# A two-layer convolution and attention network on one core: the bias network's last layer on tiles of eight keys by sixteen sums

## The chip, the cores and the metric

The kernel runs on one core of a Trainium2 chip. The metric is device time in microseconds. Three runs of the kernel before gave 2735.99 to 2738.67 us, median 2737.09. The profile is of one execution, with a span of 2735.9 us. Everything is float32.

## The reference, cut to what matters

The input is x of shape (2, 512, 32, 32). Layer 0 is deformable attention with 8 heads (16 pairs of batch and head, called groups below), each with 1024 queries and 64 keys, followed by an MLP. Layer 1 is full attention over 1024 positions. What the change touches is the bias that a small network makes for each query and key of layer 0:

```python
pos = grid_q[:, :, None, :] - grid_kv[:, None, :, :]
bias = jnp.sign(pos) * jnp.log1p(jnp.abs(pos))
bias = jax.nn.relu(bias @ cpb_w1 + cpb_b1)             # 2 -> 128
bias = jax.nn.relu(bias @ cpb_w2 + cpb_b2)             # 128 -> 128
bias = (bias @ cpb_w3 + cpb_b3).reshape(b, GROUPS, H * W, Hd * Wd)   # 128 -> 1
sim = jnp.einsum('bhid,bhjd->bhij', qh, kh) + bias
attn = jax.nn.softmax(sim, axis=-1)
```

It runs for 16 x 1024 x 64 pairs of query and key. The positions of the keys come from offsets: a 6 x 6 depthwise convolution of the queries, a GELU, a small product and a tanh.

## The kernel before, in words

**Engines.** PE is TensorE, DVE is VectorE, ACT is ScalarE, POOL is GpSimd, SP is the queue that issues most loads. Each works through its own instructions in order and waits on semaphores. The order on each engine is made by a scheduler from the order of the program; `issue_after` holds an instruction back until a named one has been issued.

**Head.** Constants are loaded on ACT's queue (kp, L170, holds an identity, W2 and w3), x on SP's. The first chunk (a chunk is 128 channels of one batch, two heads) is normalised on ACT (L235), multiplied by the query weights (psq, L243), copied to qa (L248), and its 36 taps of the depthwise convolution run on DVE (L280, L282). PE multiplies the weights of layer 1 together meanwhile (psg, L499). On POOL, `swap` (L190 to L222) reorders the columns of W2 and the entries of w3 by sign, in some 60 small steps, and makes cw2, sc and w3s.

**The loop** (L718) has 256 slots, each of four keys of one group; 16 slots make a group. In a slot:

- `st_layer1` (L585) makes h, 128 hidden channels by 4 keys by 1024 queries, on DVE (L593), up to three slots ahead, as there are three buffers.
- `st_layer2` (L603) multiplies h by W2 on PE (L610), in four parts z of 32 output channels. Each of four column groups of PE has one of the four keys, so a part is a PSUM tile of 4 keys x 32 channels by 1024 queries; there are three such tiles. ACT evicts each with bias and ReLU: parts 0 and 2 to rx (L616), 1 and 3, scaled by w3, to ua and ub (L618).
- `st_sum` (L624) forms rx * w3 + ua and rx * w3 + ub on DVE (L626). Then a DMA with addition, on POOL's queue (L628), adds ub into ua. So ua has, for each of 4 keys, 32 partial sums.
- `st_layer3` (L630) runs after every second slot for the two slots before: a matmul with w3s (L649) adds the 32 partial sums of each key into the rows of sim, a PSUM tile that a group fills in 8 such calls. At the last call of a group the product of queries and keys is added (L640).

After the last call of a group, `softmax_steps` (L657) goes on a step per slot on ACT, DVE and PE.

**Beside the loop** a generator `later` (L455) makes the features of the other seven chunks, one step per slot: `chain` (L226) computes the offsets (taps on ACT, L290, `TAPS` of them per step, and L305 on DVE) and stores their features to DRAM (fdr, L369); `sample` (L377) gathers keys and values, and writes the keys to kvz (L431 to L441). `load_tables` (L559) reads a group's features for 16 keys back from DRAM, broadcast over the partitions (fb, one buffer), every fourth slot, and `st_tables` (L570) makes two tables of them on ACT. The tables of a chunk can be loaded once its features are stored.

**After the loop** come the output projection, the MLP and layer 1 (L764 on), almost all on PE.

Of the kernel before, what the change touches and what calls it, by code (L numbers as in the profile page):

```python
# [8 lines left out]
F32 = mybir.dt.float32  # L9
AF = mybir.ActivationFunctionType  # L10
ALU = mybir.AluOpType
AX = mybir.AxisListType
PSUM = bass.MemoryType.PSUM

P = 128
# [5 lines left out]
NSL = 16  # L21
KT = 16
LAST = 2
KS = 6
# [3 lines left out]
HEAD = 3  # L28
TAPS = [36, 6, 6, 4, 4]
NU = 4  # L30
# [6 lines left out]
    ("bq", 4), ("bv", 4), ("bp", 4), ("dwb", 1), ("cb1", 1), ("cb3", 1),  # L37
    ("w1x", 1), ("w1y", 1), ("cb2", 4), ("w3", 4), ("dww", 36),
]
# [8 lines left out]
@with_exitstack  # L48
def conv_seq_kernel(ctx: ExitStack, tc: tile.TileContext, x, xt, kst, cst, vec, wsm, outw, w1, w2, wl, out):
    nc = tc.nc  # L50


    cp = ctx.enter_context(tc.tile_pool(name="cp", bufs=1))
    kp = cp.tile([P, 384], F32, name="kp")
    vs = cp.tile([P, NV], F32, name="vs")
    nc.scalar.dma_start(out=vs, in_=vec)
    xv = x.rearrange("b (k p) n -> p k b n", p=P)
    ident = kp[:, 0:128]

# [9 lines left out]
    sc = cp.tile([P, 9], F32, name="sc")  # L69
    w3s = cp.tile([P, 60], F32, name="w3s")  # L70
    nc.gpsimd.memset(w3s, 0.0)

# [66 lines left out]
    with tc.tile_pool(name="lp", bufs=2) as lp:  # L139
# [29 lines left out]
        nc.scalar.dma_start(out=cs, in_=cst)  # L169
        nc.scalar.dma_start(out=kp, in_=kst)  # L170

# [17 lines left out]

        def swap(w, of, n):  # L190
            w = w.rearrange("p (z c) -> p z c", z=4)
            t = ph.tile([P, 10, n], F32, tag="hx" if n > 1 else "swap", name=f"swap{n}")
            g, ne, a1, a3, keep, t0, t1 = t[:, 0:4], t[:, 4], t[:, 5], t[:, 6], t[:, 7], t[:, 8], t[:, 9]
            nc.gpsimd.tensor_scalar(g, w, 0.0, None, ALU.is_ge)
            for o, u, v in ((ne, g[:, 1], g[:, 3]), (a1, g[:, 0], g[:, 1])):
                nc.gpsimd.tensor_tensor(o, u, v, ALU.subtract)
                nc.gpsimd.tensor_tensor(o, o, o, ALU.mult)
            nc.gpsimd.tensor_tensor(a1, a1, ne, ALU.mult)
            nc.gpsimd.tensor_tensor(a3, ne, a1, ALU.subtract)
            nc.gpsimd.tensor_scalar(keep, ne, -1.0, 1.0, ALU.mult, ALU.add)  # L200
            for dst, src in of:
                d, v = (e.rearrange("p (z c) -> p z c", z=4) for e in (dst, src))
                nc.gpsimd.tensor_copy(d[:, 2], v[:, 2])
                nc.gpsimd.tensor_tensor(d[:, 0], v[:, 0], keep, ALU.mult)
                for z, a in ((1, a1), (3, a3)):
                    nc.gpsimd.tensor_tensor(t0, v[:, z], a, ALU.mult)
                    nc.gpsimd.tensor_tensor(d[:, 0], d[:, 0], t0, ALU.add)
                    nc.gpsimd.tensor_scalar(t1, a, -1.0, 1.0, ALU.mult, ALU.add)
                    nc.gpsimd.tensor_tensor(t1, t1, v[:, z], ALU.mult)
                    nc.gpsimd.tensor_tensor(t0, v[:, 0], a, ALU.mult)  # L210
                    nc.gpsimd.tensor_tensor(d[:, z], t0, t1, ALU.add)

        swap(kp[:, 256:384], [(cw2, kp[:, 128:256])], 32)
        w3 = vs[:, VOFF["w3"] : VOFF["w3"] + 4]
        swap(w3, [(sc[:, 0:4], w3), (sc[:, 4:8], vs[:, VOFF["cb2"] : VOFF["cb2"] + 4])], 1)
        nc.gpsimd.tensor_scalar(sc[:, 8:9], sc[:, 1:2], 0.0, 2.0, ALU.is_ge, ALU.mult)
        nc.gpsimd.tensor_scalar(sc[:, 8:9], sc[:, 8:9], 1.0, None, ALU.subtract)
        nc.gpsimd.tensor_scalar(sc[:, 0:4], sc[:, 0:4], sc[:, 8:9], None, ALU.mult)
        for z in (1, 3):
            nc.gpsimd.tensor_tensor(sc[:, 4 + z : 5 + z], sc[:, 4 + z : 5 + z], sc[:, z : z + 1], ALU.mult)  # L220
        for u in range(4):
            nc.gpsimd.tensor_copy(w3s[32 * u : 32 * u + 32, 28 + u : 29 + u], sc[32 * u : 32 * u + 32, 8:9])  # L222
        state = {}
# [153 lines left out]
        def sample(ci):  # L377
# [23 lines left out]
            for i, (b, k) in enumerate(G):  # L401
# [29 lines left out]
                for f in range(2):  # L431
                    r = slice(64 * f, 64 * f + 64)
                    d = kvz[r, f, :].rearrange("p (e i t) -> p e i t", e=2, t=4)
                    v, u = (
                        t[r].rearrange("p (i e t) -> p e i t", e=2, t=4)
                        for t in (ps[:, 0:J], sg[:, 4, f, i * J : (i + 1) * J])
                    )
                    for e in range(2):
                        nc.vector.scalar_tensor_tensor(
                            d[:, e], v[:, e], bns[r, k : k + 1], u[:, e], ALU.mult, ALU.add  # L440
                        )  # L441
# [103 lines left out]
        for _ in head:  # L545
            pass
        next(v)
        next(n)
# [5 lines left out]
        NS = NG * NSL  # L554
        tabs, h1s, sums, sims, logits = {}, {}, {}, {}, {}
        evicted, raw = {}, {}
# [46 lines left out]
        def st_layer2(s):  # L603
            h1 = h1s.pop(s)
            r = []
            for z in range(4):
                ps = zp.tile([P, 2, 512], F32, name="ps2")
                for h in range(2):
                    for q in range(4):
                        nc.tensor.matmul(  # L610
                            ps[32 * q : 32 * q + 32, h, :], cw2[:, 32 * z : 32 * z + 32],
                            h1[:, 16 * h : 16 * h + 16, q, :], start=True, stop=True,
                        )
                o = lp.tile([P, 2, 512], F32, name=("rx", "ua", "rx", "ub")[z], bufs=(3, 5, 3, 4)[z])
                if z % 2 == 0:
                    nc.scalar.activation(o, ps, AF.Relu, bias=sc[:, 4 + z : 5 + z])  # L616
                else:
                    nc.scalar.activation(o, ps, AF.Relu, bias=sc[:, 4 + z : 5 + z], scale=sc[:, z : z + 1])  # L618
                r.append(o)
                if z % 2 == 1:  # L620
                    evicted.setdefault(s, []).append(nc.cur_bb.bb.instructions[-1])
            sums[s] = r

        def st_sum(s, z):  # L624
            r = [t.rearrange("p h n -> p (h n)") for t in sums[s][z : z + 2]]
            nc.vector.scalar_tensor_tensor(r[1], r[0], sc[:, z : z + 1], r[1], ALU.mult, ALU.add)  # L626
            if z == 2 and s < NS - LAST:
                nc.gpsimd.dma_start(out=sums[s][1], in_=sums[s][3], accum_op=ALU.add)  # L628

        def st_layer3(s):  # L630
            gi, i = divmod(s // 2, NSL // 2)
            b, k, f = groups[gi]
            if i == 0:
                sims[gi] = simp.tile([P, 512], F32, name="sim")
            if i == NSL // 2 - 1:
                assert state[chain_of[b, k][0]] is None
                for h in range(2):
                    for e in range(2):
# [4 lines left out]
                        )  # L643
            parts = (1,) if s < NS - LAST else (1, 3)
            for z in parts:
                for h in range(2):
                    for e in range(2):
                        q = 64 * h + 32 * e
                        nc.tensor.matmul(  # L649
                            sims[gi][q : q + 32, :], w3s[:, 28 - 4 * i : 60 - 4 * i], sums[s + e][z][:, h, :],  # L650
                            start=(i == 0), stop=(i == NSL // 2 - 1 and z == parts[-1]),
                        )
            for e in range(2):
                sums.pop(s + e)

# [62 lines left out]
        for s in range(NS):  # L718
            if s > 0:
                st_sum(s - 1, 2)  # L720
            if s % 4 == 0 and s // 4 + 1 < 4 * NG:
                load_tables(s // 4 + 1)
# [29 lines left out]
            if tail is not None:  # L752
                with tc.issue_after(evicted[s][s % 4 == 0]):
                    tail = tail if next(tail, 0) is None else None
            if s % 2 == 1 and s >= 3:
                st_layer3(s - 3)
                if (s - 2) % NSL == NSL - 1:
                    tail = softmax_steps(s // NSL - 1)
        st_sum(NS - 1, 2)
        st_layer3(NS - 2)  # L760
        tail = softmax_steps(NG - 1)
# [417 lines left out]


def _layout(np, inputs):
    a = {k: np.asarray(v) for k, v in inputs.items()}
# [6 lines left out]
    def twice(v):  # L1189
# [7 lines left out]
        "dwb": twice(L0["off_dw_b"].reshape(DH, 1)), "cb1": L0["cpb_b1"].reshape(P, 1),  # L1197
        "cb2": np.tile(L0["cpb_b2"].reshape(4, 32).T, (4, 1)),
        "w3": np.tile(L0["cpb_w3"].reshape(4, 32).T, (4, 1)),
        "cb3": np.broadcast_to(L0["cpb_b3"].reshape(1, 1), (P, 1)),  # L1200
# [26 lines left out]
    def quarters(w):  # L1227
# [8 lines left out]
        "xt": a["x"].reshape(B, NCH, P, 8, P).transpose(4, 0, 1, 3, 2),  # L1236
        "kst": np.concatenate(
            [np.eye(P, dtype=np.float32), L0["cpb_w2"], np.broadcast_to(L0["cpb_w3"].reshape(1, P), (P, P))],
            axis=1,
        ),  # L1240
        "cst": _constants(np), "vec": vec, "wsm": wsm,
# [25 lines left out]
```

## Time and profile before

| what | us |
|---|---|
| runs, median (lowest to highest) | 2737.09 (2735.99 to 2738.67) |
| span of the profiled execution | 2735.9 |
| head, up to the first matmul of layer 2 | 41.7 |
| loop, 256 slots, to the last matmul of layer 3 | about 1948 |
| after the loop | about 746 |
| one slot of layer 2 on PE (64 records) | 6.87 |
| one call of layer 3 on PE (8 records) | 0.86 |
| DVE per slot: h, and two sums | 4.40, 2 x 1.28 |
| ACT per slot: four evictions | 2 x 1.11, 2 x 1.20 |
| addition by DMA, issue on POOL, issue to landing | 0.86, 4.6 |

A matmul in float32 appears in the trace as two records. Records of different column groups overlap: one lasts 0.59 us, but 64 of them take 6.87. A line of groups of instructions gives line, engine, operation, output and inputs, their number, the busy time and the mean of one; what follows the bar is how long the engine had been idle before them and for whom it waited. A line of stages gives the busy times in a stretch of the span.

### The profile page before, as it was taken

What the parts mean: (1) busy time and instruction counts of PE and PEld (TensorE: products, weight loads), DVE (VectorE), ACT (ScalarE), POOL (GpSimd) and SP (SyncE); (2) the same over time, 40 slices, a digit from 0 to 9 for tenths busy, and PEclk for the clock granted to TensorE, in tenths of its full rate; (3) what the DMA queues carried; (4) which work ended last, traced back from release to release, by engine and by line L of the source; (5) the groups of instructions that cost most, each with busy time, mean ns of one, the idle gap of its engine ahead of it and who ended that gap; (6) DMA issues with size and microseconds to landing.
All of it is one profiled execution on the core that took longest, in us unless ns stands there. A gap on an engine that the chain in (4) does not pass through costs nothing.

```text
span 2735.9 us, 46606 instructions
## 1 busy us (share of the span) xinstructions
PE 2718.1 (99%) x20114; PEld 983.6 (36%) x20114; DVE 2242.0 (82%) x1331; ACT 1686.5 (62%) x2164; POOL 362.8 (13%) x426
## 2 busy tenths in 40 slices
PE   9999999999999999999999999999999999999999
PEld 3332323232334333334333333333344444446455
DVE  6999999998999899999999999999864574366454
ACT  4786897788878788876876776686722021124040
POOL 3111111111111111111111111111133333000000
PEclk9999999999999999999999999999999999999999
DMA  5444444444444443444444444444331011000000
GB/s 186 92 95 91 92 100 86 87 102 100 86 87 101 101 86 82 98 93 86 86 93 90 86 90 92 86 91 92 74 139 46 32 45 46 16 16 0 31 0 31
DMA packets 64685, 214.32 MB, mean 78 GB/s; under 512 B 11104, under 2 KB 13664, under 8 KB 61792
## 3 DMA queue, kind: packets, MB, share of 16 engines
q0 software_dynamic: 36864, 135.28, 26.7%
q1 hardware_dynamic: 26752, 74.98, 7.8%
q8 instruction: 159, 2.61, 0.4%
q10 hardware_dynamic: 864, 1.07, 0.1%
q14 instruction: 46, 0.38, 0.0%
HBM read 71.59 MB, written 6.55 MB: 29 GB/s over the span
## 4 chain that ended last, share of the span: by engine, by line
PE 92%; DVE 4%; ACT 2%; issue 1%; DMA 1%; SPq 0%; DVEq 0%; ACTq 0%
PE ps L610 59%; PE sw L875 14%; PE sw L994 9%; PE sim L649 4%; PE sw L1092 2%; DVE h L593 2%; PE sw L822 1%; PE psg L499 1%; PE sim L640 0%; DVE ua L626 0%; DVE ub L626 0%; DMA fb<-fdr 0%; PE pkv L425 0%; DVE xs L830 0%; ACT rx L616 0%
## 5 line engine op out<-in xcount | busy, mean ns | idle before, releaser
L610 PE MATMUL ps<-h,cw 128*32 128x512 f32 x16384 | 1791.2, 593 | 7.4 <-ACT rx L616 5.0
L593 DVE CUSTOM_DVE_ANT_1 h<-ta,tb 128x4096 f32<-128x4096 f32 (+1 forms) x257 | 1131.8, 4404 | 85.1 <-PE ps L610 81.5
L610 PEld LDWEIGHTS ps<-h,cw 128*32 128x32 f32 x16384 | 544.1, 110 | 1215.6 <-issue 1160.9
L616 ACT ACTIVATE rx<-ps,sc 128x1024 f32<-128x1024 f32 x512 | 568.4, 1110 | 219.8 <-PE ps L610 216.6
L628 POOL DMA_DIRECT2D ua<-ub x254 | 220.0, 866 | 1697.7 <-DVE ub L626 1609.9
L618 ACT ACTIVATE ua<-ps,sc 128x1024 f32<-128x1024 f32 x256 | 308.0, 1203 | 117.1 <-PE ps L610 116.8
L618 ACT ACTIVATE ub<-ps,sc 128x1024 f32<-128x1024 f32 x256 | 307.6, 1202 | 89.2 <-PE ps L610 88.9
L626 DVE SCALAR_TENSOR_TENSOR ua<-rx,sc,ua 128x1024 f32<-128x1024 f32 x256 | 327.3, 1278 | 32.6 <-ACT ua L618 32.6
L626 DVE SCALAR_TENSOR_TENSOR ub<-rx,sc,ub 128x1024 f32<-128x1024 f32 x256 | 326.8, 1276 | 5.8 <-ACT ub L618 5.6
L875 PE MATMUL sw<-xb,w1t 128*128 128x512 f32 x448 | 193.7, 592 | 1.3 <-DVE xs L121 1.3
L875 PE MATMUL sw<-hm,w2t 128*128 128x512 f32 x448 | 193.6, 592 | 0.0
L121 DVE TENSOR_TENSOR hm<-hm,sw 128x1024 f32<-128x1024 f32 x56 | 67.6, 1220 | 112.5 <-PE sw L875 112.3
L649 PE MATMUL sim<-ua,w3s 128*32 128x512 f32 x1024 | 135.7, 594 | 0.0
L875 PEld LDWEIGHTS sw<-xb,w1t 128*128 128x128 f32 x448 | 85.1, 190 | 108.8 <-issue 105.4
L875 PEld LDWEIGHTS sw<-hm,w2t 128*128 128x128 f32 x448 | 85.2, 190 | 107.1 <-issue 106.1
L884 ACT ACTIVATE hm<-hm,vs 128x512 f32<-128x512 f32 x64 | 42.7, 713 | 129.5 <-DVE hm L121 129.5
L121 DVE TENSOR_TENSOR xs<-xs,sw 128x1024 f32<-128x1024 f32 (+1 forms) x48 | 55.6, 1171 | 74.6 <-PE sw L994 36.0
L574 ACT ACTIVATE ta<-fb,vs 128x512 f32<-128x512 f32 x64 | 88.8, 1388 | 17.7 <-DMA fb<-fdr 17.7
L994 PE MATMUL sw<-aT,vt 128*128 128x512 f32 x224 | 96.7, 593 | 0.3 <-ACT aT L1074 0.3
L909 ACT COPY hm<-sw 128x1024 f32<-128x1024 f32 x8 | 8.1, 1009 | 132.4 <-PE sw L875 132.4
L103 POOL TENSOR_TENSOR w1t<-w1t 128x512 f32<-128x512 f32 x32 | 58.4, 1844 | 112.0 <-DMA w1t<-in_w 111.4
L290 ACT ACTIVATE prod<-qa,vs 128x56 f32<-128x56 f32 (+4 forms) x180 | 64.1, 442 | 0.0
(227 smaller groups left out, 1533.3 us busy)
## 6 DMA issues: line engine op xcount, KB each, us to landing
ua<-ub POOLq DMA_DIRECT2D x254, 512.0 KB, 4.6
fb<-fdr SPq DMA_DIRECT2D x64, 512.0 KB, 4.7
w1t<-in_w SPq DMA_DIRECT2D x8, 1024.0 KB, 4.9
w2t<-in_w SPq DMA_DIRECT2D x8, 1024.0 KB, 4.9
xn<-in_x SPq DMA_DIRECT2D x8, 512.0 KB, 5.1
xnt<-in_xt SPq DMA_DIRECT2D x8, 512.0 KB, 5.7
xs<-in_x SPq DMA_DIRECT2D x16, 256.0 KB, 5.7
out<-xs SPq DMA_DIRECT2D x16, 256.0 KB, 2.1
```

The lines of the kernel that those rows point to most:

```text
L121: nc.vector.tensor_tensor(out, a, b_, op)
L290: nc.scalar.activation(dst, src, AF.Copy, scale=col("dww", 12 * m + t))
L574: nc.scalar.activation(ta.rearrange("p j x -> p x j"), fb[:, 0], AF.Identity, bias=col("cb1"), scale=col("w1x"))
L593: nc.vector._custom_dve(TENSOR_ADD_SAT, out=h1[:, y : y + step].rearrange("p y t x -> p (y t x)"), in0=a.unsqueeze(1).to_broadcast([P, ste ...
L610: nc.tensor.matmul(ps[32 * q : 32 * q + 32, h, :], cw2[:, 32 * z : 32 * z + 32], h1[:, 16 * h : 16 * h + 16, q, :], start=True, stop=True,)
L616: nc.scalar.activation(o, ps, AF.Relu, bias=sc[:, 4 + z : 5 + z])
L618: nc.scalar.activation(o, ps, AF.Relu, bias=sc[:, 4 + z : 5 + z], scale=sc[:, z : z + 1])
L626: nc.vector.scalar_tensor_tensor(r[1], r[0], sc[:, z : z + 1], r[1], ALU.mult, ALU.add)
L628: nc.gpsimd.dma_start(out=sums[s][1], in_=sums[s][3], accum_op=ALU.add)
L649: nc.tensor.matmul(sims[gi][q : q + 32, :], w3s[:, 28 - 4 * i : 60 - 4 * i], sums[s + e][z][:, h, :], start=(i == 0), stop=(i == NSL // 2 ...
L875: nc.tensor.matmul(ps[:, m, :], w[:, a, k, m * P : (m + 1) * P], x[:, b_, k, :], start=(k == 0), stop=(k == 1),)
L994: nc.tensor.matmul(ps[:, m, :], w[:, a, k, c + m * P : c + (m + 1) * P], x[b_][:, k, :], start=(k == 0), stop=(k == nk - 1),)
```

## The change

1. `_order` and `pst` are new constants; W2 is loaded transposed. Instead of sorting within groups of four channels, all 128 channels are permuted by the sign of w3: their ranks by two matmuls (`rank`), places on POOL and DVE, and a permutation matrix, `perm`. `arrange`, called after the first chain of features and before the vectors of layer 1, permutes W2, w3 and the bias on PE. Neighbouring lanes then have sums of one sign.
2. After the adding DMA of a slot, the 32 partial sums of a key become 16. `st_fold`, for even slots, adds the odd partitions of the slot's tile into the even ones. `st_join` copies the odd partitions of the odd slot's tile to the odd ones of the even slot's tile (SP), and then adds the even partitions of the odd slot's tile to them (POOL). The even slot's tile now has eight keys by sixteen sums. The fold is called at the start of the second slot after its even slot, the join one slot later.
3. `st_layer3` runs after every fourth slot, for the four slots that began seven slots before, and reads two tiles. The last four slots are not folded: five tiles are read there, in three rounds.
4. The tile ua has four buffers for even slots and is called uo, with two, for odd ones (before: five for all); ub has three (before: four). The softmax of a group begins two slots later.
5. The second chunk's taps run twelve to a step, where there were six. kvz is written in another order of keys.

The core of the diff:

```diff
-TAPS = [36, 6, 6, 4, 4]
+TAPS = [36, 12, 6, 4, 4]
...
-        nc.scalar.dma_start(out=kp, in_=kst)
+        nc.scalar.dma_start(out=pz[:, 0:413], in_=pst)
+        nc.scalar.dma_start(out=ident, in_=kst)
...
-        swap(kp[:, 256:384], [(cw2, kp[:, 128:256])], 32)
...
+        nc.gpsimd.tensor_scalar(po_, wb[:, 0:1], 0.0, None, ALU.is_ge)
+        ps = flat("rank")
+        nc.tensor.matmul(ps[:, 0:1], tri, po_, start=True, stop=True)
+        nc.tensor.matmul(ps[:, 512:513], one, po_, start=True, stop=True)
+        nc.scalar.copy(rn, ps.rearrange("p (h n) -> p h n", h=2)[:, :, 0])
...
+        def arrange():
+            ps = flat("perm")
+            nc.tensor.matmul(ps[:, 0:P], w2t, perm, start=True, stop=True)
+            for z in range(4):
+                for u in range(4):
+                    nc.tensor.matmul(
+                        ps[32 * u : 32 * u + 32, 512 + 2 * z : 514 + 2 * z], perm[:, 32 * z : 32 * z + 32], wb,
+                        start=True, stop=True,
+                    )
+            nc.scalar.copy(cw2, ps[:, 0:P])
...
-                o = lp.tile([P, 2, 512], F32, name=("rx", "ua", "rx", "ub")[z], bufs=(3, 5, 3, 4)[z])
+                name, bufs = (("rx", 3), (("ua", 4), ("uo", 2))[s % 2], ("rx", 3), ("ub", 3))[z]
+                o = lp.tile([P, 2, 512], F32, name=name, bufs=bufs)
...
-            if z == 2 and s < NS - LAST:
+            if z == 2 and s < NS - 1:
                 nc.gpsimd.dma_start(out=sums[s][1], in_=sums[s][3], accum_op=ALU.add)
+                added[0] = nc.cur_bb.bb.instructions[-1]
+        def lanes(s, i):
+            return sums[s][1].rearrange("(l e) h n -> l e (h n)", e=2)[:, i]
+        def st_fold(s):
+            with tc.issue_after(added[0]):
+                nc.gpsimd.dma_start(out=lanes(s, 0), in_=lanes(s, 1), accum_op=ALU.add)
+        def st_join(s):
+            nc.sync.dma_start(out=lanes(s, 1), in_=lanes(s + 1, 1))
+            with tc.issue_after(added[0]):
+                nc.gpsimd.dma_start(out=lanes(s, 1), in_=lanes(s + 1, 0), accum_op=ALU.add)
...
+            if s % 2 == 0 and 2 <= s < NS - 2:
+                st_fold(s - 2)
+            if s % 2 == 1 and 3 <= s < NS - 1:
+                st_join(s - 3)
...
-            if s % 2 == 1 and s >= 3:
-                st_layer3(s - 3)
-                if (s - 2) % NSL == NSL - 1:
+            if s % 4 == 3 and s >= 7:
+                st_layer3(s - 7)
+                if (s - 3) % NSL == 0:
                     tail = softmax_steps(s // NSL - 1)
```

## The prediction

> **What bounds the kernel now.** I read the busy shares first, then the chain of work that ended last, then that chain piece by piece. The chain by line:
>
> ```profile
> PE 2718.1 (99%) x20114; PEld 983.6 (36%) x20114; DVE 2242.0 (82%) x1331; ACT 1686.5 (62%) x2164; POOL 362.8 (13%) x426
> ...
> PE ps L610 59%; PE sw L875 14%; PE sw L994 9%; PE sim L649 4%; PE sw L1092 2%; DVE h L593 2%; PE sw L822 1%; PE psg L499 1%; PE sim L640 0%; DVE ua L626 0%; DVE ub L626 0%; DMA fb<-fdr 0%; PE pkv L425 0%; DVE xs L830 0%; ACT rx L616 0%
> ```
>
> PE is 99% busy and the chain lies on it for 92%; layer 3 (L649) is 4% of it. A matmul of the code appears as two records. Piece by piece, two slots of layer 2 and one call of layer 3 alternate without a gap (start, length, what):
>
> ```profile
> 74.34 0.86 PE sim L649 x8
> 75.20 13.73 PE ps L610 x128
> 88.93 0.86 PE sim L649 x8
> ```
>
> So a call of layer 3 costs PE 0.86 us, a slot of layer 2 6.87 us, and a slot of the loop on average (13.73 + 0.86) / 2 = 7.30 us. Next, who could take over from PE: stages of the loop (length, PE, PEld, DVE, ACT, POOL busy, clock, DMA share, GB/s).
>
> ```profile
> 340.00:400.00 60.00, 58.20 (x532) 17.05 (x528) 53.33 (x28) 56.96 (x104) 6.87 (x8) 1.00 0.45 101
> ...
> 700.00:760.00 60.00, 60.00 (x560) 18.07 (x552) 59.92 (x32) 51.51 (x67) 6.87 (x8) 1.00 0.44 89
> 760.00:820.00 60.00, 60.00 (x564) 19.09 (x564) 59.93 (x38) 42.94 (x42) 7.34 (x8) 1.00 0.44 90
> ...
> 1480.00:1540.00 60.00, 60.00 (x564) 18.22 (x560) 55.40 (x26) 41.39 (x38) 6.96 (x9) 1.00 0.44 89
> ```
>
> In most stages DVE has some 7% to spare, but where the features of the next chunks run beside (700 to 820, and 1000 to 1120 alike) it has nothing, and at 340 to 400 ACT has 5%. The head, from the timeline:
>
> ```profile
> 4.56 0.33 ACTq L170 DMA_DIRECT2D kp<-in_kst  x1
> 5.80 1.24 ACT L235 ACTIVATE xn<-xn,vs,bns 128x1024 f32<-128x1024 f32 x1 [3.13 <-DMA wl_s<-in_wl]
> 7.09 1.09 PE L243 MATMUL psq<-xn,ws 64*64 64x512 f32 x8 [0.26 <-ACT xn L235]
> 9.48 0.54 POOL L194 TENSOR_SCALAR swap<-kp 128x128 f32<-128x128 f32 x1 [0.76 <-DMA kp<-in_kst]
> 10.63 0.69 DVE L280 TENSOR_SCALAR acc<-qa,vs 128x64 f32<-128x64 f32 x3 [10.63 <-ACT qa L248]
> ```
>
> The head's path is psq at 7.09, qa copies, the taps on DVE from 10.63, po, then PE's weight products. The constants of kp land only at 9.45; today nobody on the path waits for them.
>
> **The Trainium skill.** "TensorEngine Tiling (Array Packing)", Instruction Overhead, says that a matmul has some 60 cycles of its own and that one of width 1 takes as long as one of width 60; used for the tiny matmuls. "DMA: Bandwidth & Descriptors", Anatomy of one DMA, gives 2.0 us plus bytes / 436e3, 3.2 us for 512 KB; the adds of L628 take 4.6 us (median; 8.3 longest), so the trace's is used. The same section says that the wait before a DMA is made by the issuing sequencer: POOL and SP stand still. "Trainium Kernel Development and Optimization", Key Constraints, says that all queues share the 16 DMA engines; the page shows both queues together at 44% in the loop.
>
> **The change, part by part.** The sum is made against this span, 2735.9 us; the median of the runs is 1.2 us above it.
>
> (1) *Layer 3.* Before: 127 calls of 0.86 and a last one of 1.72 (two rounds) = 110.9 us. After: 63 calls of 0.86 and a last one of three rounds, the third on two of four column groups but as long, 2.58 = 56.8. All on PE's path: **-54.1**. A pair of slots now averages 14.16 instead of 14.59 us.
>
> (2) *Adding lanes.* Per two slots the change adds a fold (64 partitions, 256 KB) and a joining add on POOL's queue, and a copy of 256 KB on SP's. A packet of L628 takes 0.34 us, eight per engine; a fold is four, 1.35 us. DMA work per two slots: 0.44 x 14.6 = 6.4, plus 2 x 1.35, plus about 0.8 for the copy = 9.9 of 14.16 us, 70%: no bound. Does it land in time? Count from the start A of the add of slot s+1. The fold is queued behind it, its packets follow the add's, and it lands at about A+6 (4.6 + 1.35). SP then copies: 2.2 us was the store of 256 KB (L1124), so A+8.5. The next add starts at A+7.1; the join waits on POOL for the copy, starts at A+8.5, its packets follow that add's, and it lands at A+13. On POOL only the add of the slot after that (A+14) is behind it. The odd slots' tile (two buffers) is written again four slots after; an add starts 6.5 us after its slot's last matmul, so that eviction comes at A+18.4: 5.4 us of slack. Layer 3, seven slots behind, has 9. Reads by layer 3 are thus hidden behind later slots. At four places SP has the feature stores (4.0 us for four issues) and a table load ahead of a copy: taken at **+1** in all, 0 to +8; no gain, since nothing is removed from these queues.
>
> (3) *The head.* Rank matmuls now stand on PE ahead of psq, and they need the new constants, issued where kp was (206 KB against 192): they land near 9.5 instead of being wanted at 7.09. With the matmuls psq starts near 9.85: +2.75 to the whole head (ACT's one further DMA issue, xn 0.4 us later, is inside it, as are the DVE and POOL steps on place and rank: six and three of 0.2 to 0.3 us, over before the taps at 13.4). Then, after the first weight product, 34 records of perm matmuls: not in this trace. Below: 34 x 60 cycles, 0.85 us by the Tiling page's price at the 2.4 GHz that "Trainium Kernel Development and Optimization", NeuronCore Architecture, gives, an estimate; above: 34 x 0.115 (L523, 128x1) = 3.9. I take 2.0, as four column groups can overlap. One idle 0.66 us (PE waiting for h at 42.76) is filled: **+4.1**, 2.5 to 6.5. The about 60 small POOL steps that go were beside PE: nothing. The new ACT copies and POOL steps for sc end long before the first eviction at 44.6.
>
> (4) *Twelve taps a step for chunk two.* Six took 1.85 us on ACT. A slot has four evictions of 1.1 and now 3.7 of taps, 8.1 against 7.1: three slots, so about +3, less the slack of three PSUM buffers, +2. On the other side, before, ACT waited 3.5 us at 265 for the tables of that chunk and PE lost 1.5; three slots earlier, that goes. **+0.5**, -2 to +4.
>
> (5) *What PE's speed meets.* DVE's work per slot is unchanged, but 60 us of before become 58.3. Windows of 60 us with DVE above 58.3 (160, 400, 700, 760, 1000, 1060, 1240) exceed it by 8.2 us together. Some is carried: h is ready 8 to 14 us ahead, but the sums may fall back only about 2.6 us before their rx buffer is wanted, and they already fall back by up to 2.2. I lose 6 (0 to 8.2), and 1 (0 to 6) where ACT's taps fill it, as at 340 to 400: **+7**.
>
> (6) *Waits.* Sums and evictions name more semaphores, 21 ns each on DVE, taken while the step before runs: 0. The end of the loop keeps its order, and the last add is prompt as DVE has no more h to make: 0. kvz is only written in another order: 0.
>
> Sum: -54.1 + 1 + 4.1 + 0.5 + 7 = -41.5, so 2694.4 in this span and **2695.5** in the runs.
>
> **The rivals.** *A. Hardly anything is given back:* DVE's lead carries all of (5), the copies are never late. For it: PE idles only 7 us in the loop. Head at 2.5, taps at -2: -53.6, about 2683. Chance 0.07. *B. DVE and ACT give back more:* (5) at 14, head 6.5, taps 4, queues 5: -24.6, about 2712, or up to 2725 if the loop's DVE-bound stages grow. For it: three stages at 99.9%. Chance 0.12. *C. Slower: the lane transfers set the pace.* Place: ACT's eviction into the odd slots' tile (L642 after), waiting for the join; its order on ACT stops PE once three PSUM buffers are full, some 2.2 us on. It decides when the join lands after A+18.4+2.2 = A+20.6; each us beyond is paid once per four slots, 64 times, so the gain is gone at A+21.3. If fold and join took 7.5 us (the longest add took 8.3) and the copy 5.7 (median of the loads of xs), the join would land at A+22.5: +122, about 2817. Against it: the median add is 4.6 and the DMA engines are at 44%. Chance 0.07. *D. The change doesn't do what it says* (calls of layer 3 don't get fewer or longer ones result): the order of the built program shows half the calls, of the same shape; 2737 within 5. Chance 0.03.
>
> **How the numbers follow.** Main case 0.71, B 0.12, A 0.07, C 0.07, D 0.03. The main case spans 2684 to 2709 by the bounds of (2) to (5); stretched to 2712 for half of B, the range 2684 to 2712 leaves out about 0.2. About 0.2% (5.5 us) is what a measurement of this kernel can tell from no change: faster by more 0.90, within 0.03, slower 0.07.
>
> **What would show it.** Layer 3 in the groups with about 524 records of the same length instead of 1032, and 2% of the chain; psq near 9.9 and the first layer 2 matmul near 46; DVE and ACT named more often as what PE waited for, between 160 and 1300 only, and stages after 1300 at the full 14.16 us per two slots; DMA share near 0.7; ACT's eviction into uo never waiting for a DMA. Wrong if that eviction waits, if the head moves by more than 6.5, or if the stages after 1300, where DVE has room, don't get shorter by 3%.

## The result, and the profile after

| | before | after |
|---|---|---|
| runs, median (lowest to highest), us | 2737.56 (2735.99 to 2738.67) | 2698.03 (2695.95 to 2698.86) |
| span of the profiled execution, us | 2735.9 | 2694.2 |
| first matmul of layer 2, us | 41.7 | 45.2 |
| slots 4 to 252 of the loop, us | 1883.0 | 1840.2 |
| from slot 252 to the end, us | 777.9 | 777.2 |

The ratio is 0.9855 (95% interval 0.9838 to 0.9872). The prediction was 2695.5 us in the runs and 2694.4 in the span. There are four runs of each; the profiled execution of the kernel after, 2695.95 us, is the fastest of its four.

First the page of the kernel after, its busy shares and its chain of work by line:

```profile
PE 2668.7 (99%) x19644; PEld 961.0 (36%) x19644; DVE 2239.4 (83%) x1337; ACT 1681.3 (62%) x2166; POOL 575.6 (21%) x625
...
PE ps L633 57%; PE sw L928 14%; PE sw L1047 9%; PE sim L698 2%; PE sw L1145 2%; DMA ua<-ua 1%; DMA ua<-uo 1%; PE psg L521 1%; PE sw L875 1%; ACT prod L312 1%; ACT rx L640 1%; DVE h L616 1%; ACT ub L642 1%; PE sim L682 0%; ACT sx L745 0%
```

PE is still 99% busy. Layer 3 (now L698) went from 4% of the chain to 2%, and ACT's taps (prod L312) and its scaling of the softmax (sx L745) are new among the lines listed. So are the transfers (ua<-ua and ua<-uo, 1% each), which the first experiment answers. The waits of PE for an eviction, before and after (total us, times, longest us):

```profile
PE ps L610 <- ACT rx L616: 5.0, 4, 2.7
PE ps L610 <- ACT ua L618: 1.5, 1, 1.5
```

```profile
PE ps L633 <- ACT rx L640: 14.2, 13, 2.7
```

These are nearly all the stops of PE in the loop. Adding up every record of PE between slots 4 and 252 accounts for the -42.75 us: the products into sim take 51.8 us less, PE's stops 7.9 more (14.6 against 6.7), and layer 2's own records (L633, formerly L610) 1.2 more. In stages (length, then PE, PEld, DVE, ACT, POOL busy, clock, DMA share, GB/s):

```profile
340.00:400.00 60.00, 54.65 (x512) 15.93 (x504) 55.81 (x30) 59.85 (x121) 12.30 (x14) 1.00 0.65 140
700.00:760.00 60.00, 60.00 (x564) 20.57 (x560) 60.00 (x39) 46.90 (x54) 14.91 (x17) 1.00 0.68 145
...
1480.00:1540.00 60.00, 60.00 (x564) 18.60 (x560) 57.18 (x28) 42.94 (x45) 14.10 (x16) 1.00 0.69 146
```

From 340 to 400 PE stops for 5.35 us and ACT has 0.15 us left. From 700 to 760 DVE is full, yet PE doesn't stop. So the time given back lies mostly with ACT, while the prediction had put 6 of 7 us on DVE. The timeline of the largest stop shows how (start, busy, what; in brackets the idle time before):

```profile
356.49 1.18 ACT L642 ACTIVATE ub<-ps,sc 128x1024 f32<-128x1024 f32 x1
357.58 2.58 ACT L312 ACTIVATE prod<-qa,vs 128x112 f32<-128x112 f32 x6
...
360.06 0.33 ACT L736 ACTIVATE sx<-sx,mx 128x64 f32<-128x64 f32 x1
360.30 0.18 ACT L736 ACTIVATION_READ_ACCUMULATOR sx<-sx,mx 128x1 f32 x1
...
361.39 1.09 ACT L640 ACTIVATE rx<-ps,sc 128x1024 f32<-128x1024 f32 x1
362.38 1.18 ACT L642 ACTIVATE uo<-ps,sc 128x1024 f32<-128x1024 f32 x1
362.53 1.92 PE L633 MATMUL ps<-h,cw 128*32 128x512 f32 x16 [2.71 <-ACT rx L640]
```

Six taps and four exponentials stand one behind the other on ACT, 3.8 us, before the eviction that PE needs, which takes 1.09 itself. PE went on for 2.2 us after the eviction before had ended (357.67 to 359.82), on the PSUM tiles that were free, and then stopped. Two tables (L597, L604) had gone just before. The second large stop has another start:

```profile
828.69 0.18 DVE L731 TENSOR_SCALAR mx<-mx 128x16 f32<-128x16 f32 x1
...
828.95 1.28 ACT L736 ACT_TABLE_LOAD   x1 [3.64 <-DVE mx L731]
...
830.92 1.09 ACT L640 ACTIVATE rx<-ps,sc 128x1024 f32<-128x1024 f32 x1
...
832.07 2.96 PE L633 MATMUL ps<-h,cw 128*32 128x512 f32 x16 [2.52 <-ACT rx L640]
```

ACT stands 3.64 us for the maxima of a softmax, which DVE, full in this stage, made late. The eviction that needs nothing from DVE is queued behind them.

The head, from the timeline of the kernel after:

```profile
4.71 0.33 ACTq L175 DMA_DIRECT2D pz<-in_pst  x1
...
9.01 0.35 PE L209 MATMUL rank<-pwork,pz 128*128 128x1 f32 x2 [2.11 <-POOL bz L511]
...
9.52 1.37 PE L265 MATMUL psq<-xn,ws 64*64 64x512 f32 x8
...
27.36 0.43 PE L229 MATMUL perm<-vs,pwork 128*32 128x2 f32 x32
27.63 1.92 PE L536 MATMUL psu<-wl_s,bz 128*32 128x512 f32 x16
...
45.20 2.35 PE L633 MATMUL ps<-h,cw 128*32 128x512 f32 x20
```

The matmuls of the ranks wait, and psq stands behind them: 9.52 instead of 7.09. The bracket names POOL, but the load of pz had landed at 8.88, and in each of the nine traces with this head the first of these matmuls starts 0.13 to 0.14 us after that landing (8.88 to 9.90), so it is the load that they wait for. The permutation takes 0.6 us (27.04 to 27.63).

The new transfers, from the list of DMA issues (KB each, median us from issue to landing): the two forms of the add, the fold, the copy and the joining add.

```profile
ua<-ub POOLq DMA_DIRECT2D x128, 512.0 KB, 4.8
uo<-ub POOLq DMA_DIRECT2D x127, 512.0 KB, 5.0
...
ua<-ua POOLq DMA_DIRECT2D x126, 256.0 KB, 6.3
ua<-uo SPq DMA_DIRECT2D x126, 256.0 KB, 2.4
ua<-uo POOLq DMA_DIRECT2D x126, 256.0 KB, 4.0
```

Counted as in the prediction from the start A of the second slot's add (medians), the fold lands at A+7.0, the copy at A+9.7, the join at A+15.1, and the eviction into the odd slots' tile starts at A+19.2. The median slack is 3.9 us, the least 0.07. In four slots (at 810, 981, 1010 and 1452 us) that eviction starts 0.07 us after the join has landed, so it waited; ACT had been idle for 1.8 us in all before the four, 1.2 of it before the last. PE stopped at none of them.

### The profile page after: what moved, and what is told of

It reads as the page before. It is cut to its first block, busy times and chain, and to the rows that moved or that the text cites. A ratio compares the mean times of both kernels' runs of the same rounds, so it can differ in the third digit from the quotient of the medians.

```text
span 2694.2 us, 47017 instructions
## 1 busy us (share of the span) xinstructions
PE 2668.7 (99%) x19644; PEld 961.0 (36%) x19644; DVE 2239.4 (83%) x1337; ACT 1681.3 (62%) x2166; POOL 575.6 (21%) x625
## 4 chain that ended last, share of the span: by engine, by line
PE 88%; ACT 4%; DMA 3%; issue 2%; DVE 2%; POOL 0%; ACTq 0%; DVEq 0%; POOLq 0%; SPq 0%
PE ps L633 57%; PE sw L928 14%; PE sw L1047 9%; PE sim L698 2%; PE sw L1145 2%; DMA ua<-ua 1%; DMA ua<-uo 1%; PE psg L521 1%; PE sw L875 1%; ACT prod L312 1%; ACT rx L640 1%; DVE h L616 1%; ACT ub L642 1%; PE sim L682 0%; ACT sx L745 0%
## 5 line engine op out<-in xcount | busy, mean ns | idle before, releaser
L633 PE MATMUL ps<-h,cw 128*32 128x512 f32 x16384 | 1784.1, 593 | 14.6 <-ACT rx L640 14.2
L633 PEld LDWEIGHTS ps<-h,cw 128*32 128x32 f32 x16384 | 536.2, 110 | 1231.3 <-issue 1130.1
L652 POOL DMA_DIRECT2D ua<-ub x128 | 114.7, 896 | 726.9 <-DVE ub L650 698.8
L652 POOL DMA_DIRECT2D uo<-ub x127 | 117.6, 926 | 388.0 <-DVE ub L650 317.5
L642 ACT ACTIVATE ua<-ps,sc 128x1024 f32<-128x1024 f32 x128 | 154.0, 1203 | 57.1 <-PE ps L633 56.8
L642 ACT ACTIVATE uo<-ps,sc 128x1024 f32<-128x1024 f32 x128 | 153.9, 1202 | 40.1 <-PE ps L633 38.0
L650 DVE SCALAR_TENSOR_TENSOR ua<-rx,sc,ua 128x1024 f32<-128x1024 f32 x128 | 164.1, 1282 | 16.4 <-ACT ua L642 16.3
L669 POOL DMA_DIRECT2D ua<-uo x126 | 108.4, 861 | 321.2 <-DMA ua<-uo 306.1
L650 DVE SCALAR_TENSOR_TENSOR uo<-rx,sc,uo 128x1024 f32<-128x1024 f32 x128 | 164.1, 1282 | 11.8 <-ACT uo L642 11.7
L664 POOL DMA_DIRECT2D ua<-ua x126 | 152.7, 1212 | 5.3 <-DMA ua<-ub 4.2
L937 ACT ACTIVATE hm<-hm,vs 128x512 f32<-128x512 f32 x64 | 42.6, 713 | 129.5 <-DVE hm L121 129.5
```

The source lines that it names most:

```text
L633: nc.tensor.matmul(ps[32 * q : 32 * q + 32, h, :], cw2[:, 32 * z : 32 * z + 32], h1[:, 16 * h : 16 * h + 16, q, :], start=True, stop=True,)
L664: nc.gpsimd.dma_start(out=lanes(s, 0), in_=lanes(s, 1), accum_op=ALU.add)
L669: nc.gpsimd.dma_start(out=lanes(s, 1), in_=lanes(s + 1, 0), accum_op=ALU.add)
```

## The experiments

Medians of 4 to 7 runs each; the kernel before, run beside them, had medians of 2735.99 to 2737.78 us, so a difference of 2 us between kernels that didn't run beside each other says little.

**Are the transfers hidden?** All folds and joins taken out, so that the bias lacks most of its sums:

```diff
-            if s % 2 == 0 and 2 <= s < NS - 2:
-                st_fold(s - 2)
-            if s % 2 == 1 and 3 <= s < NS - 1:
-                st_join(s - 3)
```

> The changed kernel without folds and joins; layer 3 reads unfolded tiles, so the bias is wrong: the lane sums of half the lanes are left out of it. Changed kernel: 2698.0 us. Theory (the loop's give-back of some 10 us is ACT and DVE falling behind a faster PE, transfers are hidden): 2695 to 2699, PE's waits in the loop as before, 340 to 400 us still with ACT at 59 us of 60. Rival (the give-back is the transfers: fewer free DMA engines, POOL and SP blocked, the eviction into uo waiting): 2687 to 2690.

Measured: 2696.76 us (2696.18 to 2699.24), ratio 0.9857 (0.9843 to 0.9872). The stage from 1480 in this kernel:

```profile
1480.00:1540.00 60.00, 60.00 (x564) 18.61 (x560) 57.17 (x27) 42.46 (x40) 6.98 (x8) 1.00 0.47 95
```

The DMA share fell from 0.69 to 0.47, POOL's busy time from 14.10 to 6.98, and the time stayed, inside the theory's range. PE's stops in the loop are as before, 14.4 us against 14.6. The transfers are hidden.

**Does PE set the pace?** Every call of layer 3 done twice, the second time with zero weights:

```diff
-            parts = [[(w, sums[s + 2 * e][1])] for e in range(2)]
+            parts = [[(w, sums[s + 2 * e][1]), (wz, sums[s + 2 * e][1])] for e in range(2)]
```

> The changed kernel with every call of layer 3 made a second time, with weights of zero, so the result is the same: 63 calls of 0.86 us more and two or three rounds more in the last, some 56 us of PE. Theory (PE sets the pace, with slack of ACT and DVE where PE was slowed): 2698 plus 56 less the some 10 us that were given back: 2742 to 2746, that is before plus the head's 3.5 and the 1 to 2 of the rest. Rival (lane transfers cost the 10 us): 2752 to 2755, since they stay. If PE did not set the pace: 2700 to 2715.

Measured: 2744.90 us (2743.24 to 2746.23), 46.9 more than the kernel after: the gain is gone. The calls are on the path: from slot 4 to 252 the records of sim take 53.0 us more. The loop gets only 46.4 longer there, because PE's stops fell from 14.6 to 9.5 us, as a slower loop leaves ACT more time, and layer 2's own records took 1.5 less. At this pace, nearly that of the kernel before (1886.6 us for these slots, against 1883.0), PE still stops 2.8 us more than there: this part isn't the pace, but may be the places at which the features and the softmax now meet, as taps and softmax were both moved by the change. That wasn't tested apart.

**The gain alone.** The kernel before with half of its layer-3 calls left out, so that half of the keys lack their bias:

```diff
             parts = (1,) if s < NS - LAST else (1, 3)
+            if i in (1, 3, 5, 6):
+                parts = ()
```

> The kernel before with four of the eight calls of layer 3 of each group left out (half of the bias is left out); no lane transfers, old head, taps as before. 64 calls of 0.86 us less, 55.0 us. Theory: ACT and DVE give back some 9 us here too, so 2690 to 2693. Rival (give-back belongs to the transfers): 2682 to 2685.

Measured: 2690.97 us (2689.09 to 2692.16), ratio 0.9833 (0.9816 to 0.9849). Without any new transfer, permutation or change of taps, the loop from slot 4 to 252 gets 45.5 us shorter, and the runs are in the theory's range. The records of sim take 52.4 less; PE's stops rise from 6.7 to 10.4, of which 2.1 are waits of layer 3 for the adding DMA, which the kernel before has too, and layer 2's own records take 3.3 more, which wasn't traced further. So a loop made faster in another way gives back 6.9 us without the new transfers.

**The head.** The matmuls of the ranks held behind psq and the first weight product, in a PSUM tile of their own; their constants are loaded later on the same queue:

```diff
-        nc.scalar.dma_start(out=pz[:, 0:413], in_=pst)
...
         nc.scalar.dma_start(out=ws[:, P:1024], in_=wsm[:, P:1024])
+        nc.scalar.dma_start(out=pz[:, 0:413], in_=pst)
...
-            nc.tensor.matmul(ps[:, 0:1], tri, po_, start=True, stop=True)
+            with tc.issue_after(newest(mybir.EngineType.PE)):
+                nc.tensor.matmul(ps[:, 0:1], tri, po_, start=True, stop=True)
...
         marks.append(newest(mybir.EngineType.PE))
+        rank()
```

> The changed kernel with the rank matmuls behind psq and the first part of psg on PE (in the gap before po), their constants issued after the query weights and the identity much later. Theory (rank in front of psq costs the head 2.4 to 3.5 us): psq starts near 7.1 instead of 9.5, the first matmul of layer 2 near 42.8, 2694.5 to 2696. Rival (the head is held by the features' way through DRAM, or the place steps now delay th on DVE by 1.5): 2697 to 2699.

Measured: 2694.56 us (2694.22 to 2694.69). This is in the theory's range. psq starts at 7.58, layer 2 at 42.50. The head's loss came from two tiny matmuls in PE's queue that wait for a load. The edit moves that load as well, but xn, which psq multiplies, was ready at 7.53 in the kernel after too, so what psq stood for there, until 9.52, were the ranks.

**Twelve taps a step.** The kernel after with TAPS as before:

```diff
-TAPS = [36, 12, 6, 4, 4]
+TAPS = [36, 6, 6, 4, 4]
```

> The changed kernel with six taps a step for chunk two, as before. Theory: the wait of ACT for that chunk's tables comes back (PE lost 1.5 us to it), now with the copies ahead in SP's queue so up to 4, and the overload of ACT by taps around 140 to 170 us (PE idle some 1.4 there) goes: 2697 to 2701. Rival (twelve taps a step cost more than they give): 2692 to 2696. Rival (without them SP is blocked behind the tables and the copies come late): 2705 or more.

Measured: 2703.31 us (2701.21 to 2703.99), above the theory's range. One stage of it, and the same of the kernel after:

```profile
240.00:300.00 60.00, 56.10 (x499) 15.79 (x492) 52.86 (x27) 42.37 (x50) 13.22 (x15) 0.94 0.66 139
```

```profile
240.00:300.00 60.00, 60.00 (x576) 18.75 (x572) 59.10 (x32) 47.15 (x55) 14.59 (x17) 1.00 0.74 164
```

With six taps the features of the second chunk are late: PE stops for 3.9 us, and its records run slow after that (clock 0.94). The kernel before lost 1.5 us at this place; the faster loop needs the tables sooner. Slots 4 to 32 take 211.0 us, against 205.8 in the kernel after, and the runs are 5.3 us apart: so much twelve taps are worth here.

**Fewer taps where taps meet the softmax.** The third chunk's taps four to a step:

```diff
-TAPS = [36, 12, 6, 4, 4]
+TAPS = [36, 12, 4, 4, 4]
```

> The changed kernel with four taps a step for the third chain of chunks instead of six. Theory (340 to 400 us is bound by ACT, taps of two chunks at once meeting the softmax): PE idles there 5.4 us, some 3 of them go; 2694.5 to 2696.5. Rival (later features of these chunks then come late, or meet the softmax elsewhere): 2697 to 2702.

Measured: 2697.56 us (2695.99 to 2698.49), in the rival's range and not told from the kernel after. Slots 32 to 48 got 1.3 us shorter, 88 to 104 and 124 to 144 about 2.5 each, but 104 to 124 took 3.5 more and 144 to 164 2.7 more. What was won at one place was lost at another; that the longer chain met other work there is argued, not shown.

**DVE through rx.** The prediction's step (5): sums that fall behind keep rx from being evicted. A fourth buffer of rx, which fits only where xn shares a tile with bz; the control has the sharing alone:

```diff
-            xn = ph.tile([P, HW], F32, name="xn")
+            xn = ph.tile([P, HW], F32, tag="xnt", name="xn")
```

> Control for the next: the changed kernel with x and its transpose, xn and xnt, in one buffer, which makes room for a fourth rx. Theory: these loads are early enough, 2697 to 2699; rival: SP is blocked behind the later load, 2700 or more.

Measured: 2696.32 us (2696.24 to 2697.85), a little below the theory's range, and inside the spread of the kernel after.

```diff
-                name, bufs = (("rx", 3), (("ua", 4), ("uo", 2))[s % 2], ("rx", 3), ("ub", 3))[z]
+                name, bufs = (("rx", 4), (("ua", 4), ("uo", 2))[s % 2], ("rx", 4), ("ub", 3))[z]
```

> The control with a fourth buffer of rx. Theory (where DVE is full, 700 to 820 and 1000 to 1120 us, the sums fall back until rx is wanted again and ACT waits 12 us for it): those waits go, DVE is carried over to idle stages, 3 to 6 us less than the control. Rival (PE's stops come from ACT alone; DVE's lag is only passed on to the folds and the eviction into uo): within 1.5 us of the control.

Measured: 2696.98 us (2696.51 to 2697.36). ACT's wait for DVE's sums in the loop, in the kernel after, then with four buffers, and last PE's waits with four:

```profile
ACT rx L640 <- DVE ub L650: 12.3, 10, 2.6
```

```profile
ACT rx L640 <- DVE ub L650: 0.5, 1, 0.5
```

```profile
PE ps L633 <- ACT rx L640: 13.9, 12, 2.7
```

The wait that the prediction blamed was there, and is gone; PE stops as long as before (14.3 us in the loop, 14.4 in the control). ACT waited for DVE at moments at which PE didn't need it.

**Exponentials spread out.** Two per slot in eight slots, alone and with the ranks behind psq:

```diff
-                if a % 2 == 1:
+                if a % 2 == 1 or gi < NG - 2:
                     yield
```

> The kernel after, with the softmax's exponentials of all but the last two groups spread over eight slots, two per slot, where four per slot ran in four slots. Nothing is removed. Theory (what is given back between slots 32 and 252 is ACT alone, where taps of the features and exponentials fall into the same slots): ACT's load in the fullest slots falls by two exponentials, PE's waits for the evictions to rx fall clearly below the 14 us of the kernel after, slots 32 to 48 take 125 us or less (127.9 in the kernel after), and the runs 2692 to 2695.5 us. Rival (the work only meets the taps of other slots, as it did with four taps a step): the waits stay at 12 to 15 us, and the runs 2696 to 2699 us.

Measured: 2696.61 us (2695.84 to 2698.51). The waits of PE:

```profile
PE ps L633 <- ACT rx L640: 11.1, 15, 2.0
...
PE ps L633 <- DVE kvz L461: 2.5, 1, 2.5
```

Neither side's numbers held whole. The stop of 2.71 us became 2.00 and that of 2.52 became 1.32, but a new one of 2.5 us came up at 1137 behind a step of the features, the slots 32 to 48 took 126.3 us, where the theory asked for 125 or less, and the time is the rival's.

> Both changes together: the matmuls of the ranks behind psq on PE, and the exponentials over eight slots. The two lie in different stretches (the head, and the loop from slot 32), so the theory adds them: 3.5 us from the head on top of the run with eight slots alone; first matmul of layer 2 at about 42.5 us, and the runs 2689 to 2692.5 us. Rival (the exponentials bring nothing): 2693.5 to 2696 us, as with the ranks alone.

Measured: 2691.81 us (2690.57 to 2693.39): inside the theory's range, 2.8 below the ranks alone. The slots 32 to 48 take 124.5 us, against 129.5 with the ranks alone, in one profile each. But the stops are hardly what was won: of the 4.1 us by which slots 4 to 252 got shorter, PE's stops are 0.8, and 3.4 are records that ran slowly after two stops of the ranks alone and don't here (last section).

**Exponentials mostly left out:**

```diff
-                for i in range(n):
+                for i in range(n if a == 0 or gi >= NG - 2 else 0):
                     nc.scalar.activation(
```

> The kernel after without most of the softmax's exponentials: for all groups but the last two only the first of eight blocks of queries is put through Exp, so the attention of layer 0 is not the reference's. An exponential costs ACT 0.34 us and 0.19 us for its accumulated sum, so 14 of them are 7.5 us less for ACT in each pair of groups. Theory (PE's stops between slots 32 and 252 come where ACT has exponentials on top of taps): PE's waits for the evictions to rx fall from 14 us to at most 5 us, slots 32 to 48 take 122 to 124 us (127.9 in the kernel after), and the runs 2685 to 2690.5 us. Rival (the taps alone, or DVE and the products of the features, make the stops): waits of 10 us or more, and 2694 to 2698 us.

Measured: 2694.43 us (2693.28 to 2694.99); the theory's 2685 to 2690.5 failed, and the rival's 2694 to 2698, with waits of 10 us or more, held.

PE's waits:

```profile
PE ps L633 <- ACT rx L640: 12.0, 13, 2.5
```

The stop at 360 fell from 2.71 to 1.38 us, and the one before it from 1.14 to 0.46. Those at 398, 635 and 643 stayed: there the taps meet the softmax's scaling, not its exponentials. The one at 830 stayed too, at 2.55, as ACT waits for DVE's maxima all the same. So the exponentials are one of several pieces.

**The softmax moved away from the taps**, with the ranks behind psq. Nothing is left out; a list lets a group's softmax go on after the short one of the next group:

```diff
+            for _ in range({1: 10, 3: 18, 5: 4, 7: 8}.get(gi, 0)):
+                yield
             sm = f_pool.tile([P, 8, 2], F32, name="sm", bufs=2)
...
-                    tail = softmax_steps(s // NSL - 1)
+                    tails.append(softmax_steps(s // NSL - 1))
```

> The kernel with the ranks behind psq, and with the softmax of the first four pairs of groups held back behind its maxima by 10, 18, 4 and 8 slots, so that its exponentials and scalings fall into slots in which ACT has no taps, and so that the exponentials don't stand on ACT waiting for a maximum that DVE makes late. Work and number of instructions are the same. Theory (PE stops where ACT's queue holds two kinds of work beside the loop in one slot, or an instruction that waits for DVE, ahead of an eviction): of the stops after slot 32, 11.6 us in the kernel after, at most 4 are left; PE's waits for the evictions to rx are at most 6 us in all, and the runs 2682 to 2688 us. Rival (each kind alone is enough, and delayed work only meets other slots, as with four taps or with eight slots of exponentials): waits of 9 us or more, and 2690 to 2695 us.

Measured: 2689.12 us (2688.17 to 2690.51), ratio 0.9823 (0.981 to 0.9837): the fastest of all, between the two ranges. PE's waits, and the stage from 340:

```profile
PE ps L638 <- ACT rx L645: 9.0, 15, 1.3
PE ps L638 <- DVE kvz L463: 2.8, 2, 2.6
```

```profile
340.00:400.00 60.00, 58.20 (x544) 17.11 (x533) 56.17 (x32) 54.85 (x85) 14.11 (x16) 1.00 0.61 132
```

Of the stops near 360, 398, 635, 643 and 830 (8.7 us in the kernel after) the last four are gone, and the one near 360 is 1.27 us instead of 2.71: taps behind two tables are left there, without exponentials. This says that these stops came from the two kinds of work on ACT, or from the wait for the maxima. But others of up to 1.1 us came in their place, and one of 2.6 for a step of the features, as the rival said: PE's waits for the evictions to rx are 9.0 us, where the theory asked for 6 at most. All stops in the loop are 12.0 us, against 14.4 with the ranks alone. Of the 6.1 us by which slots 4 to 252 got shorter, that is 2.4, and 3.4 are the records that ran slowly after two stops of the ranks alone (last section). So the shorter stops themselves are less than half of what was won. Where ACT's least loss lies stays open.

## Why the prediction was right, and where it was not

- **(1) Layer 3, -54.1: right.** For slots 4 to 252 the same working gives 62 calls of 0.86, 53.3; the records of sim took 51.8 less. With layer 2's 1.2 more, 2.7 us are missing, and no run shows why. Some calls were torn apart by the scheduler, their eight records standing in two pieces, but in the last experiment, where none is, the records of sim and of layer 2 together take only 0.6 us less (without the slow ones of the last section). Doubling the calls (experiment two) shows that they lie on PE's path.
- **(2) Transfers, +1: fits, but isn't told from nothing.** Without them the runs are 1.3 us apart, inside their spread. The stations came later than worked out (join A+15.1 for A+13): the fold lands 1.0 us later, and the join takes 0.9 longer behind the copy. The DMA share of 0.69 is the 70% worked out. That the eviction into uo would never wait was wrong: it waited in four slots, at no cost to PE. "DMA: Bandwidth & Descriptors" (Anatomy of one DMA) says, and this trace agrees, that the wait stands on the issuing sequencer: POOL's joins waited 306 us for copies, with nothing urgent behind them.
- **(3) Head, +4.1: 3.5 in this profile.** psq at 9.52 (9.85 predicted). The permutation was mis-sized: 0.6 us for 2.0. Its lower bound from "TensorEngine Tiling (Array Packing)" (Instruction Overhead) was 0.85, an estimate; the measurement is below, 32 of the 34 records being issued to four column groups. This profile was lucky: in the eight other traces with this head psq begins at 10.05 to 10.95 and layer 2 at 45.7 to 47.6, so the head's usual cost is 4.0 to 5.9 us, within the range of 2.5 to 6.5. Part of it comes after psq, where PE ran slowly (last section); the prediction has no such term.
- **(4) Twelve taps, +0.5: right in size against the kernel before.** The new stops at 156 and 164 are 0.66 + 0.77 us, and the 1.54 at 270 went. What the step didn't see is that without it the faster loop would have lost 5.3 us more.
- **(5) Falling behind, +7 (DVE 6, ACT 1): the size was right, the cause was not.** Outside (4) PE's stops grew by 8.0 us. The sums do fall back (the add starts up to 12.2 us after the end of its slot's last matmul, 6.1 as a rule; before, 9.5 at most), but a fourth rx buffer took ACT's wait for them away and gained nothing. The stops are ACT's own queue: of the ten above 0.6 us inside the loop, nine have taps, or weights of the features, ahead of an eviction, most of them with tables, exponentials or scalings beside, and one, of 2.5 us, has exponentials that wait for DVE's maxima: of DVE's 6 us only that is found, and on another way. Some 5 of the 7.9 us by which all stops grew go when the loop is slowed to the old pace (experiment two). The prediction gave ACT 1 us, as it looked for ACT's load in whole stages; a stop is made within one slot.
- **(6) Waits, 0**, and no other cost showed: from slot 252 on the two traces differ by 0.7 us.

The sum met the span within 0.2 us, and that is luck in two ways. The profiled execution is the fastest of its four; the median of the runs is 2.5 us above the predicted 2695.5. And small errors have both signs: slots 4 to 252 gave 2.0 less than worked out, mostly in (1), while the head came 0.6 lower, the first four slots 0.9 shorter than their one call of layer 3 tells (0.66 of it is the filled idle that (3) had counted in the head), and the end 0.7 shorter.

Two of the three signs of being wrong came up. The eviction into uo waited, as told under (2). And the slots 164 to 252, which start at 1305 us in the kernel before, got 2.7% shorter (652.9 to 635.1 us), not 3: the prediction's own 14.59 to 14.16 is 2.9%, and leaves out the other products that PE makes in these slots. Neither touches the mechanism of (1).

Of the rivals, C is out by the join's A+15.1 against A+21.3, and D by the records (504 of them for 63 calls, of the same length). A is out by the stops, and B's size wasn't reached.

## What to carry to other kernels

When the engine that sets the pace gets faster, look for what is given back where side work is queued in one slot on the engine that frees its buffers, and for slots in which two kinds of side work meet, not at the busy share of a stage. Moving such work opens new stops elsewhere, so count all of them. A wait that the profile names isn't yet a loss: a buffer that takes it away tells whether PE cared. Transfers on engines with room cost nothing that could be measured here, as the slot that reuses their tile came after them in all but four cases; tiny matmuls whose data comes late don't belong ahead of the first product of a chain.

## What the hardware showed that was not expected

After a stop of 2 us or more PE sometimes runs its next matmuls slowly: records of up to 1.06 us instead of 0.59, for some 3 to 6 us, which costs 1.4 to 3.0 us on top of the stop. It followed 12 of the 22 stops above 1.9 us in the loops of the fourteen traces of this case, and no shorter one; kernels that have the same two stops show it after one of them or after both. After the stop at 829.5 of the kernel after, 20 records took 3.84 us, where they take 2.15 at full pace; after the longer one at 359.8 none was slow. So a stop's price is not its length alone.

The trace names what goes with it. In the stretches below, one after each of these two stops (the clock is the third number from the end), the granted clock reads 0.50 after the first and 1.00 after the second:

```profile
832.80:836.20 3.40, 3.40 (x20) 0.87 (x16) 3.35 (x4) 2.08 (x2) 0.00 (x0) 0.50 1.03 195
362.50:365.90 3.40, 3.37 (x32) 1.07 (x36) 2.85 (x5) 3.40 (x6) 0.85 (x1) 1.00 1.03 195
```

In all 12 cases the clock reads 0.50 for 3.4 us, or 6.8 after the longest stop (3.9 us, with six taps), and nowhere else between slots 4 and 252. The head has it too: in the nine traces in which the ranks stand ahead of psq, the clock reads 0.50 for 3.4 us (two traces, layer 2 at 45.2 and 45.7) or for 6.8 (seven, layer 2 at 46.4 to 47.6), beginning at 7.7 to 10.6 us; in the five others it doesn't. In the loop the ranks alone have two such stretches, at 361 and 832 us, which cost 3.4 us together; the two runs that spread or move the softmax on top of that have none. Why the clock falls after one stop and not after another stays open.
